# A state-space block and a mixture of experts on one core: the first block's rows spread by TensorE, softplus from the absolute value, the branch ahead of the projection

## The chip, the cores and the metric

The kernel runs on one core of a Trainium2 chip. The metric is device time in microseconds, the median of several executions. One further execution was recorded by the hardware profiler; every profile line below is from that one. The engines are PE (TensorE, matrix products), DVE (VectorE), ACT (ScalarE), POOL (GpSimd) and SP (SyncE, which here issues nearly all transfers).

## The reference

The input x is 4 sequences of 1024 tokens with 128 channels. Two layers follow, each added to its input and normalised. The first is a selective state-space layer:

```python
xz = einsum('bld,ed->ble', x, in_proj_w)          # 512 = 2 x 256 channels
xb, z = xz[..., :256], xz[..., 256:]
xb = silu(conv_b + sum over 4 taps of xpad[:, k:k+Lq] * conv_w[:, k])
proj = einsum('bld,ed->ble', xb, x_proj_w)        # 33 rows: dt_in, 16 of B, 16 of C
dt = softplus(dt_in * dt_w[:, 0] + dt_b)
dA = exp(dt[..., None] * A)                       # A = -exp(A_log), 16 states a channel
x_scaled = (xb * dt)[..., None] * Bp[..., None, :]
h[t] = dA[t] * h[t-1] + x_scaled[t]               # written as an associative scan
y = einsum('bldn,bln->bld', h, Cp) + xb * D_param
y = layernorm(y) * ln_g + ln_b;  y = y * silu(z);  out = y @ out_w.T
```

The second is a causal attention with 16 heads of 8 channels, then a mixture of 16 experts (128 to 512 to 128, gelu, two experts a token, limited capacity).

## The kernel before

**Two plans.** The kernel is written as a list of operations, each with a due time `v`, the engines that could do it and an estimated duration. `Plan.schedule` (L194) simulates the engines: when one is free it takes, among the operations whose inputs are done and whose buffers are free, the one with the lowest `v`. `Plan.run` (L337) emits the instructions in that order. Engines take their instructions strictly in order, so a misjudged order makes an engine wait on the chip, while idle time in the plan itself is not emitted. An ACT operation that needs another function table than the loaded one gets 100 added to its `v`. Where the plan sees a gap of 800 ns or more on PE while an accumulation group is open, it sends groups of four matmuls by zeros (`fill`, L1556), one group for each 550 ns of gap.

`plan_a` (`before_branch`, L1451) holds the work ahead of a branch; the second plan (`mild_path`, L1518) all the rest. The branch tests one number, `mild`: a bound on the attention scores that is worked out from the weights (`pn`, `nrm`, `pbound`, `most`, L1475 to L1499, with a power on POOL and due times 9 and 10). The other side of the branch is a slower path that is not run here.

**Fronts.** Tokens are taken in eight halves of a sequence, 512 tokens each. `front(f, v, step)` (L1403) computes for one half, channels on partitions: `conv` (four taps as matmuls with the weights `w_tap`) and its Silu `xb`; `zmm` and its Silu `sz`; `xproj` and a copy `proj`; the product `dtmm` with `w_dt`. Then softplus for each of two groups of 128 channels: `dtmin` on DVE (add the bias, limit to 40), Exp, Ln(1 + .) on ACT, and the maximum with the argument on DVE (`dt`); then `u` = xb times dt. All of xb, sz, the B and C rows (`bc_d`), dt and u are written to DRAM. Front 0 stands in `plan_a`, the seven others in the second plan with due times 18 to 112. `front_w` matrices, A_log and the small vectors are loaded at the very start, A_log by ACT's queue (L1504).

**Scans.** `scans(u)` (L1652) takes a unit of 512 (at the end 256) tokens. For a block `m` of 128 channels it reads dt and u back so that 32 channels lie on 128 partitions, each repeated for 4 of the 16 states (`u_sp`, `dt_sp`, four transfers of 256 KB each), and the B and C rows repeated over channels. For each of four state groups: `uB` on DVE, four decays `da` = Exp(a_neg * dt) on ACT (five buffers), four `scan` on DVE, `hC` on DVE, and `py` on PE, which sums over states.

**The rest.** `norm_and_inputs` (L1733) does the layer norm, the gate and the output product, and q, k, v for attention in three bf16 parts each; its powers (`rs_pow`, `lnx_pow`) run on POOL. `attention` (L1804) runs at a lag of 60 to 90 in due time behind the scans; its tiles lie over the fronts' buffers, so it starts when the last front is done. Five of its tiles get 64 rows cleared on POOL (`pad`, L2025, due at 100). `post` (L1868) ends the layer and prepares token rows (`xrow`, with a token number from POOL in the last column); `route` sends rows to experts; the experts follow.

The operation helpers of class `Emit` record every operation under a few lines: L390 is every matmul, L417 every activation, L437 every tensor_tensor, L463 every scan, L450 a tensor_scalar of two operations (`dtmin` among them), L457 a scalar_tensor_tensor, L368 every plain transfer.

Of the kernel before, what the change touches and what calls it, by code (L numbers as in the profile page):

```python
# [9 lines left out]
F32 = mybir.dt.float32  # L10
# [8 lines left out]
P = 128  # L19
# [36 lines left out]
TABLE = 1283  # L56
# [81 lines left out]
class Op:  # L138
    __slots__ = ("v", "engs", "emit", "deps", "succ", "left", "ready", "start", "end", "done", "eng", "allocs",
                 "uses", "table", "name", "wire", "seq", "opens", "closes")  # L140


class Plan:
# [17 lines left out]
    def add(self, v, engs, emit, outs, ins, name="", table=None, wire=0, free=(), after=()):  # L161
# [3 lines left out]
        op.opens = op.closes = None  # L165
        op.start = op.end = op.done = op.eng = None
# [27 lines left out]
    def schedule(self):  # L194
# [65 lines left out]
        times, queued = [0.0], {0.0}  # L260

# [7 lines left out]
        while n_left:  # L269
# [8 lines left out]
            while again:  # L278
                again = False
                for e in engines:  # L280
# [3 lines left out]
                    for op in waiting[e]:  # L284
# [6 lines left out]
                        if e == "ACT" and op.table and op.table != table:  # L291
                            v += 100.0
                        if best is not None and (v, op.seq) >= best[:2]:
                            continue
# [23 lines left out]
                    op.end = t + dur  # L318
                    op.done = op.end
# [17 lines left out]
    def run(self):  # L337
        order = self.schedule()
        last, ready, groups = 0.0, False, {}
        with self.tc.manual_schedule():  # L340
            for op in order:
                if op.eng == "PE":
                    gap = op.start - last
                    if ready and groups and gap >= FILL_GAP:
                        view = next(iter(groups.values()))
                        for _ in range(int(gap / FILL_STEP)):
                            self.fill(view)
                    last = op.end
                op.emit(op.eng)
                ready = ready or op is self.fill_after  # L350
                if op.opens is not None:
                    groups[id(op.opens.buf)] = op.opens
                if op.closes is not None:
                    groups.pop(id(op.closes.buf), None)


class Emit:
# [12 lines left out]
    def pe(self, v, calls, share=1, name="", group=None, last=False):  # L370
        nc = self.nc
        dur, outs, ins = 0.0, [], []
        for kind, out, lhsT, rhs, start, stop in calls:
# [7 lines left out]
            dur += one / 0.92 / share  # L381
            outs.append(out)
# [9 lines left out]
        op = self.p.add(v, {"PE": dur}, emit, outs, ins, name)  # L392
        if group is not None:
            op.opens, op.closes = (None, group) if last else (group, None)
# [34 lines left out]
    def _dve(self, v, emit, outs, ins, cols, per=1.0, fixed=None, name="", pool=False):  # L429
        if fixed is None:  # L430
            fixed = 125 if any(x.psum for x in outs + ins) else 62
        return self.p.add(v, {"POOL" if pool else "DVE": (fixed + per * cols / 0.96) * (2.2 if pool else 1)}, emit, outs, ins, name)

    def tt(self, v, out, a, b, op, pool=False, name=""):
        eng = self.nc.gpsimd if pool else self.nc.vector
        fixed = 600 if op == ALU.pow else None
# [41 lines left out]
    def memset(self, v, out, value, pool=False, name=""):  # L478
        eng = self.nc.gpsimd if pool else self.nc.vector
        return self._dve(v, lambda e: eng.memset(out.real(), value), [out], [], out.cols, name=name, pool=pool)  # L480
# [15 lines left out]
def mamba_then_moe_block_kernel(ctx: ExitStack, tc: tile.TileContext, a: dict, out: bass.AP):  # L496
# [847 lines left out]

    plan_a = Plan(nc, tc)
# [36 lines left out]
    conv_b, dt_b = small("f_conv_b", [P, NC2]), small("f_dt_b", [P, NC2])  # L1382
# [8 lines left out]
    def fronts_of(p, e, n_dt):  # L1391
# [9 lines left out]
        W = dict(w_in=fx(w_in), w_tap=fx(w_tap), w_xp=fx(w_xp), w_dt=fx(w_dt), conv_b=fx(conv_b), dt_b=fx(dt_b))  # L1401

        def front(f, v, step):  # L1403
# [9 lines left out]
            xb = []  # L1413
            for c in range(NC2):
                pt = p.new(pool["bank"])
                e.pe(v + step, [
# [4 lines left out]
                e.act(v + 2 * step, t, pt, AF.Silu, bias=W["conv_b"][:, c : c + 1], name="xb")  # L1421
                e.dma(v + 7 * step, fx(chan["xb"][f])[c * P : (c + 1) * P, :], t, name="xb_d")
                xb.append(t)
            for c in range(NC2):
                pt = p.new(pool["bank"])
                e.pe(v + 2 * step, [("mm", pt, W["w_in"][:, DI + c * P : DI + (c + 1) * P], xT[:, NTAP - 1 :], True, True)], name="zmm")
                t = p.new(pool["sz"])
                e.act(v + 2 * step, t, pt, AF.Silu, name="sz")
                e.dma(v + 6 * step, fx(chan["sz"][f])[c * P : (c + 1) * P, :], t, name="sz_d")
            pt = p.new(pool["bank"])  # L1430
            e.pe(v + 3 * step, [("mm", pt, W["w_xp"][:, c, :], xb[c], c == 0, c == NC2 - 1) for c in range(NC2)], name="xproj")
            proj = p.new(pool["proj"])
            e.act(v + 3 * step, proj, pt, AF.Copy, name="proj")
            e.dma(v + 4 * step, fx(bc_h[f]).rearrange("s g i t -> (s g i) t"), proj[1 : 1 + 2 * NS, :], name="bc_d")
            for c in range(NC2):
# [3 lines left out]
                b1 = W["dt_b"][:, c : c + 1]  # L1439
                e.ts(v + 4 * step, ex, pt, b1, DT_MAX, ALU.add, ALU.min, name="dtmin")  # L1440
                e.act(v + 5 * step, ex, ex, AF.Exp, name="sp_exp")
                e.act(v + 5 * step, ex, ex, AF.Ln, bias=fx(one_col), name="sp_ln")
                dt = p.new(pool["dt"])
                e.stt(v + 6 * step, dt, pt, b1, ex, ALU.add, ALU.max, name="dt")
                e.dma(v + 6 * step, fx(chan["dt"][f])[c * P : (c + 1) * P, :], dt, name="dt_d")
                u = p.new(pool["u"])
                e.tt(v + 6 * step, u, xb[c], dt, ALU.mult, name="u")
                e.dma(v + 6 * step, fx(chan["u"][f])[c * P : (c + 1) * P, :], u, name="u_d")
        return front

    def before_branch():  # L1451
        p, e = plan_a, ea
        fx = p.fixed
        for t, value in ((mean_col, 1.0 / DI), (one_col, 1.0), (neg_half, -0.5)):
            e.memset(0, fx(t), value, name="memset")
        def load(v, t, src, queue="SP"):
# [11 lines left out]
        load(2.2, w_dt, fx(a["dt_w"]))  # L1468
        load(2.3, dt_b, fx(a["dt_b"]).rearrange("(n p) -> p n", p=P))
        for k in range(NTAP):  # L1470
            e.tt(2, fx(w_tap)[:, k, :], fx(w_in)[:, 0:DI], fx(conv_w)[:, :, k], ALU.mult, name="w_tap")
        front = fronts_of(p, e, 2)
        front(0, 0.5, 2.5)

        pn = ps.single[0][:, 0:8].rearrange("p (t s g) -> p t s g", t=2, s=2)  # L1475
        for s, w in enumerate((wq_pad, wk_pad)):
            sqw = fx(bnd[s])
            e.ts(3, sqw, fx(w), fx(ln1_w), None, ALU.mult, name="sqw")
            e.tt(3, sqw, sqw, sqw, ALU.mult, name="sqw")
            for g in range(GQ):  # L1480
                e.pe(9, [("mm", fx(pn)[:, 0, s, g : g + 1], sqw[:, g, :], fx(one_col), True, True),
# [754 lines left out]
```

## Time and profile before

| what | value |
|---|---|
| timed executions, median of 3 | 1115.01 us (1114.6 to 1119.04) |
| profiled execution, its own time | 1093.94 us |
| its span, first to last instruction | 1092.1 us |
| mean granted clock of PE | 0.914 |
| first scan begins | 47.60 us |
| last scans end | about 768 us |
| first expert matmul | 920.39 us |
| last transfers and norm | 1047 to 1092 us |

Times inside the execution count from the span's start. In the lines of the timeline the columns are start, duration, engine, line, operation, output and inputs; "x4" counts instructions, and the bracket holds the idle time of that engine ahead of them and what ended it. In lists of waits the numbers are microseconds in total, times, and the longest.

### The profile page before, as it was taken

Reading aid. Unit: us, or ns where it says so; the run is one execution under the profiler, and the core shown is the slowest. Engines: PE = TensorE matmul, PEld = TensorE weight load, DVE = VectorE, ACT = ScalarE, POOL = GpSimd, SP = SyncE. Lnnn points to the kernel's source line nnn. Section 1 sums busy time; section 2 is a strip of 40 time slices with the busy share of each in tenths; the row PEclk is TensorE's granted clock in tenths of the full one; section 3 lists DMA queues with packets and bytes.
Section 4 is the critical chain, followed back from the end, with each engine's and each line's share of the span. In section 5 each row is a group of like instructions: output and inputs, shape, how many; then the busy total and the mean of one; then the engine's idle time right before and its main releaser. Section 6 shows DMA issues by size and latency. Waiting matters only on the chain.

```text
span 1092.1 us, 16985 instructions
## 1 busy us (share of the span) xinstructions
PE 891.0 (82%) x6090; PEld 446.7 (41%) x6136; DVE 793.4 (73%) x1390; ACT 708.1 (65%) x1069; POOL 233.4 (21%) x337
## 2 busy tenths in 40 slices
PE   6378879577899999899999899999889964999910
PEld 2123324224334324543433543434455532777710
DVE  2477889998999999999999999999524221111146
ACT  3376687354898897788799679898656742334311
POOL 2020001300001000182100263000060303555532
PEclk9589989778999999899999989999999975999965
DMA  3776587575754644374555466345943302322162
GB/s 104 254 189 217 180 285 247 175 217 179 233 134 136 215 136 131 123 226 145 181 152 148 123 189 169 91 144 159 306 125 94 109 12 78 119 86 68 40 170 84
DMA packets 152757, 168.65 MB, mean 154 GB/s; under 512 B 23635, under 2 KB 105814, under 8 KB 152534
## 3 DMA queue, kind: packets, MB, share of 16 engines
q1 hardware_dynamic: 146262, 158.63, 48.4%
q0 software_dynamic: 4096, 8.43, 2.2%
q8 instruction: 50, 0.82, 0.3%
q10 hardware_dynamic: 2304, 0.40, 0.2%
q14 instruction: 45, 0.37, 0.1%
HBM read 110.20 MB, written 57.21 MB: 153 GB/s over the span
## 4 chain that ended last, share of the span: by engine, by line
PE 48%; DVE 24%; ACT 10%; DMA 7%; issue 7%; POOL 2%; SPq 1%; DVEq 0%; ACTq 0%; POOLq 0%
PE bank L390 25%; PE pair L390 20%; DVE arena L463 10%; DVE arena L437 10%; ACT arena L417 8%; DVE arena L457 2%; PE bank L388 2%; SPq L368 1%; DMA arena<-in_fc_w_dram 1%; DMA arena<-q_parts 1%; DVE smalls L487 1%; DMA q_parts<-halves 1%; POOL smalls L437 1%; DMA eout<-rt_full 1%; DMA k_parts<-halves 1%
## 5 line engine op out<-in xcount | busy, mean ns | idle before, releaser
L417 ACT ACTIVATE arena<-pair 128x1024 f32<-128x1024 f32 (+2 forms) x336 | 299.1, 923 | 66.7 <-PE pair L390 57.0
L437 DVE TENSOR_TENSOR arena<-arena 128x2048 f32<-128x2048 f32 (+2 forms) x155 | 305.7, 1991 | 11.9 <-DMA arena<-u_h 11.9
L417 ACT ACTIVATE arena<-arena,f_a_neg 128x512 f32<-128x512 f32 (+1 forms) x288 | 187.8, 675 | 82.4 <-DVE arena L463 68.2
L390 PE MATMUL pair<-arena 128*128 128x256 bf16 (+3 forms) x821 | 184.0, 309 | 25.1 <-ACT arena L417 17.6
L437 POOL TENSOR_TENSOR smalls<-smalls,neg_half 128x4 f32<-128x4 f32 (+2 forms) x35 | 54.0, 1544 | 598.5 <-DVE smalls L448 531.7
L390 PE MATMUL bank<-arena,vp 128*32 128x256 f32 (+3 forms) x1728 | 165.6, 465 | 2.9 <-ACT arena L412 1.3
L463 DVE TENSOR_TENSOR_SCAN arena<-arena,state 128x512 f32<-128x512 f32 (+1 forms) x160 | 160.9, 1054 | 0.0
L463 DVE TENSOR_TENSOR_SCAN arena<-arena 128x512 f32<-128x512 f32 x128 | 150.1, 1209 | 0.1
L390 PEld LDWEIGHTS <-arena 128*128 128x128 bf16 x864 | 79.0, 98 | 155.3 <-issue 132.9
L2010 POOL DMA_INDIRECT xin<-xrow,rt_put x64 | 83.1, 1299 | 82.0 <-issue 34.6
L390 PE MATMUL bank<-arena,f_sel 128*32 128x512 f32 x512 | 72.6, 643 | 30.2 <-DVE arena L437 30.0
L390 PE MATMUL pair<-mask_k,identb 128*128 128x128 bf16 x512 | 95.3, 220 | 1.6 <-issue 0.8
L417 ACT ACTIVATE arena<-pair,b 128x512 f32<-128x512 f32 x64 | 40.5, 684 | 71.4 <-PE pair L390 71.4
L390 PE MATMUL pair<-xT,f_w_tap 128*128 128x512 f32 x128 | 64.2, 651 | 21.7 <-DMA xT<-in_xT_dram 17.8
L2111 POOL DMA_INDIRECT eout<-arena,to x64 | 61.3, 957 | 67.5 <-DVE arena L437 56.8
L390 PEld LDWEIGHTS bank<-arena,vp 128*32 128x32 f32 x1728 | 38.2, 109 | 59.7 <-issue 45.2
L417 ACT ACTIVATE arena<-arena,smalls 128x128 f32<-128x128 f32 x73 | 30.3, 483 | 49.3 <-DVE smalls L457 45.1
L390 PEld LDWEIGHTS bank<-arena 128*128 128x128 f32 x512 | 59.8, 192 | 5.6 <-issue 4.3
L390 PE MATMUL bank<-arena 128*128 128x128 f32 x512 | 61.2, 277 | 0.5 <-ACT arena L417 0.4
L437 DVE TENSOR_TENSOR arena<-bank,arena 128x512 f32<-128x512 f32 (+1 forms) x25 | 16.7, 666 | 60.6 <-PE bank L390 60.6
L388 PE MATMUL bank<-ident,arena 128*128 128x128 f32 x256 | 42.3, 291 | 21.5 <-DMA arena<-xin 15.9
L390 PE MATMUL pair<-arena,arena 128*128 128x512 f32 x128 | 59.4, 608 | 0.0
(184 smaller groups left out, 1082.7 us busy)
## 6 DMA issues: line engine op xcount, KB each, us to landing
arena<-k_parts SPq DMA_DIRECT2D x52, 288.0 KB
arena<-bc_h SPq DMA_DIRECT2D x56, 256.0 KB
arena<-dt_h SPq DMA_DIRECT2D x56, 256.0 KB
arena<-u_h SPq DMA_DIRECT2D x56, 256.0 KB
arena<-in_fc_w_dram SPq DMA_DIRECT2D x32, 256.0 KB
q_parts<-halves SPq DMA_DIRECT2D x21, 384.0 KB
k_parts<-halves SPq DMA_DIRECT2D x21, 384.0 KB
arena<-q_parts SPq DMA_DIRECT2D x28, 288.0 KB
```

The costliest lines, as they stand in the source:

```text
L368: return self.p.add(v, {queue: 460}, lambda e: engine.dma_start(out.real(), in_.real()), [out], [in_], name, wire=wire, after=after)
L388: nc.tensor.transpose(out.real(), lhsT.real(), rhs.real())
L390: nc.tensor.matmul(out.real(), lhsT=lhsT.real(), rhs=rhs.real(), start=start, stop=stop)
L417: nc.scalar.activation(out.real(), in_.real(), func, scale=real(scale), **kw)
L437: return self._dve(v, lambda e: eng.tensor_tensor(out.real(), a.real(), b.real(), op), [out], [a, b], out.cols, fixed=fixed, name=name, po ...
L457: return self._dve(v, lambda e: nc.vector.scalar_tensor_tensor(out.real(), a.real(), real(s), b.real(), op0, op1), [out], self._views(a, s ...
L463: return self._dve(v, lambda e: nc.vector.tensor_tensor_scan(out.real(), d0.real(), d1.real(), real(init), ALU.mult, ALU.add), [out], self ...
L487: self._dve(v, lambda e: nc.vector.bn_stats(s.real(), x.real()), [s], [x], 128, name=name + "_bn")
L2010: inst = nc.gpsimd.indirect_dma_start(out=dst.real()[:, :], out_offset=bass.IndirectOffsetOnAxis(ap=idx.real(), axis=0), in_=src.real(), i ...
L2111: inst = nc.gpsimd.indirect_dma_start(out=eo_d.real()[:, :], out_offset=bass.IndirectOffsetOnAxis(ap=idx.real(), axis=0), in_=src.real(), ...
```

## The change

The change has these parts.

1. `front` is split into `conv_half` (conv, xb, zmm, sz) and `dt_half` (xproj to u). Front 0's `conv_half` stays ahead of the branch; its `dt_half` moves behind it, where `adopt` takes over the two xb buffers. The chain of `mild` gets due times of 1.8 to 2.9.
2. Softplus is max(x, 0) + ln(1 + exp(-|x|)). The bias dt_b becomes a row of `w_dt`, with a matching row of ones that the copy of `proj` adds; `dtmin` goes, and an Abs on ACT takes its place.
3. Block m = 0 of unit 0 no longer goes through DRAM: eight matmuls by a 0/1 matrix (`wide`) spread dt and u over partitions into PSUM. The first state group's decays and `uB` read PSUM; eight copies (`spread_c`, ACT or DVE) fill the tiles for the other three groups. Front 1's conv waits for the last of these matmuls and its gates for the last of these decays.
4. A_log is loaded by SP's queue; its Exp waits for the second gate of front 0.
5. The planner: a function of another table must have been ready for 3 us before it is taken (`HOLD`); PE is counted at half speed in windows of 3413 ns that follow one with little work (`Clock`); the costs of a power and a memset on POOL change; fillers are also sent before the first attention product, into a spare bank, in both plans.
6. The pads are due at 150 instead of 100, and the token column is written ahead of `x2`.

```diff
-TABLE = 1283
+TABLE, HOLD = 1283, 3000
+SPAN, ENOUGH = 3413.0, 3000.0
...
+class Clock:
...
+    def slow(self, k):
+        return self.work.get(k - 1, 0.0) < ENOUGH
...
+    def fill(self, t, gap, n):
+        for i in range(n):
+            k = int((t + (i + 0.5) * gap / n) / SPAN)
+            self.work[k] = self.work.get(k, 0.0) + 512.0
...
                         if e == "ACT" and op.table and op.table != table:
                             v += 100.0
+                            if t < op.ready[e] + HOLD:
+                                wake(op.ready[e] + HOLD)
+                                continue
...
+                    if e == "PE":
+                        gap = t - last
+                        if ready and (groups or spare) and gap >= FILL_GAP:
+                            op.fillers = int(gap / FILL_STEP)
+                            clock.fill(last, gap, op.fillers)
+                            op.filled = next(iter(groups.values()), None)
+                        spare = spare and op.name != "av"
+                        op.end = last = clock.end(t, dur, op.work)
...
-        fixed = 600 if op == ALU.pow else None
+        fixed = 620 + 63 * out.cols if op == ALU.pow else None
...
+    def filler(p, spare):
+        def fill(view):
+            n = spare.cols if view is None else view.cols
+            to, some = (spare if view is None else view).real(), some_b.unsqueeze(1).to_broadcast([P, n // P, P])
+            for j in range(4):
+                nc.tensor.matmul(to[32 * j : 32 * j + 32, :], lhsT=zero_b, rhs=some, start=view is None, stop=view is None)
...
-            e.act(v + 3 * step, proj, pt, AF.Copy, name="proj")
+            e.act(v + 3 * step, proj, pt, AF.Identity, bias=fx(ident)[:, 1 + 2 * NS : 2 + 2 * NS], name="proj")
...
-                b1 = W["dt_b"][:, c : c + 1]
-                e.ts(v + 4 * step, ex, pt, b1, DT_MAX, ALU.add, ALU.min, name="dtmin")
-                e.act(v + 5 * step, ex, ex, AF.Exp, name="sp_exp")
+                e.act(v + 4 * step, ex, pt, AF.Abs, name="sp_abs")
+                e.act(v + 5 * step, ex, ex, AF.Exp, scale=-1.0, name="sp_exp")
                 e.act(v + 5 * step, ex, ex, AF.Ln, bias=fx(one_col), name="sp_ln")
                 dt = p.new(pool["dt"])
-                e.stt(v + 6 * step, dt, pt, b1, ex, ALU.add, ALU.max, name="dt")
+                e.stt(v + 6 * step, dt, pt, 0.0, ex, ALU.max, ALU.add, name="dt")
...
-        front(0, 0.5, 2.5)
+        conv_half(0, 0.5, 2.5)
...
-        e.act(21, a_all, a_all, AF.Exp, name="a_all")
+        e.act(21, a_all, a_all, AF.Exp, name="a_all").deps.add(conv_half.last[1][1])
...
+        xb_first = [adopt("xb") for _ in range(NC2)]
+        first = dt_half(0, 0.0, 2.0, xb_first, kept=(0,))
...
+                    if spread:
+                        wide = new("tmp", "wide")
+                        e.copy(1, wide.rearrange("p (m i) -> p m i", i=NI), fx(ident).unsqueeze(2).to_broadcast([P, P, NI]), name="wide")
+                    for j in range(J if spread else 0):
+                        lhsT = wide[:, j * P : (j + 1) * P]
+                        for src, dst, k in ((first[0][0], dts[j], 0), (first[0][1], us[:, j, :], 1)):
+                            pb = new("bc")
+                            mm = e.pe(12 + 0.1 * j + 0.05 * k, [("mm", pb, lhsT, src, True, True)], name="spread")
+                            if k:
+                                e.tt(12 + 0.1 * j, h[:, j, :], pb, bt[g], ALU.mult, name="uB")
+                            else:
+                                d_first.append(new("da"))
+                                ex = e.act(12 + 0.1 * j, d_first[j], pb, AF.Exp, scale=fx(a_neg)[:, j, 0:1], name="da")
+                            e.act(14 + j, dst, pb, AF.Copy, dve=True, name="spread_c")
+                    for conv, gate in second_front if spread else ():
+                        conv.deps.add(mm)
+                        gate.deps.add(ex)
...
-                e.memset(100, rest[64:P, :], 0.0, pool=True, name="pad")
+                e.memset(150, rest[64:P, :], 0.0, pool=True, name="pad")
```

`Clock.end`, not shown, divides a matmul's duration by one half while `slow` holds.

## The prediction

> **What bounds the kernel now.** I read the page first, then busy time by stage, the timeline of the start, and the waits of VectorE (DVE) while the projections run.
>
> ```profile
> span 1092.1 us, 16985 instructions
> PE 891.0 (82%) x6090; PEld 446.7 (41%) x6136; DVE 793.4 (73%) x1390; ACT 708.1 (65%) x1069; POOL 233.4 (21%) x337
> ```
>
> No engine is full on average, so the stages decide (columns: PE, PEld, DVE, ACT, POOL busy, granted PE clock, DMA share, GB/s):
>
> ```profile
> 0.00:45.00 45.00, 18.59 (x48) 8.17 (x48) 10.65 (x38) 14.36 (x19) 6.49 (x26) 0.75 0.47 146
> 75.00:132.00 57.00, 48.46 (x139) 18.27 (x138) 45.45 (x50) 42.66 (x56) 0.20 (x2) 0.92 0.58 193
> ...
> 304.00:390.00 86.00, 80.28 (x577) 33.31 (x584) 85.51 (x94) 74.78 (x110) 6.53 (x4) 1.00 0.53 160
> ...
> 800.00:860.00 60.00, 55.92 (x586) 33.76 (x585) 19.83 (x106) 39.95 (x56) 22.68 (x42) 1.00 0.36 105
> ```
>
> Until 45 us nobody is busy: a latency chain. From 304 to 734 DVE is 95% to 99% busy in every stage (85.51 of 86 in the one shown): the scans. After their end near 770 PE works off the attention that is left (55.92 of 60), then the experts. Attention of a block needs its scans, and the experts need the last attention; so what DVE gains before attention starts (about 255) should reach the end whole. The start:
>
> ```profile
> 17.84 0.69 ACT L417 ACTIVATE arena<-pair,f_conv_b 128x512 f32<-128x512 f32 x1 [7.12 <-PE pair L390]
> 18.55 1.28 ACT L409 ACT_TABLE_LOAD   x1
> 19.84 0.31 ACT L417 ACTIVATE arena<-arena 128x128 f32<-128x128 f32 x1
> 20.17 1.28 ACT L417 ACT_TABLE_LOAD   x1
> 21.46 0.69 ACT L417 ACTIVATE arena<-pair,f_conv_b 128x512 f32<-128x512 f32 x1
> ...
> 37.51 2.48 SPq L368 DMA_DIRECT2D arena<-u_h  x4
> ...
> 45.21 2.29 DVE L437 TENSOR_TENSOR arena<-arena 128x2048 f32<-128x2048 f32 x1 [11.86 <-DMA arena<-u_h]
> ...
> 47.60 4.57 DVE L463 TENSOR_TENSOR_SCAN arena<-arena 128x512 f32<-128x512 f32 x4
> ```
>
> The two gates of the convolution are torn apart by an Exp that needs another table, and DVE then waits 11.86 us for rows that were written to DRAM (dt from 31.08, u from 32.34) and are read back spread out. DVE's waits from 45 to 205 us:
>
> ```profile
> DVE arena L450 <- PE pair L390: 14.7, 4, 5.6
> DVE arena L437 <- DMA arena<-u_h: 11.9, 1, 11.9
> DVE arena L457 <- ACT arena L417: 3.9, 4, 2.1
> DVE arena L450 <- ACT arena L417: 2.7, 1, 2.7
> ```
>
> L450 is `dtmin`, one small pass that stands on DVE ahead of the scans and waits for a projection that PE has not done.
>
> **The start, step by step.** The convolution still ends near 17.8: the weight load and w_tap (8.96 to 11.17) gate it, and no edit shortens those. Gates at 17.84 and 18.5, done 19.1 instead of 22.15, since Exp of A_log now waits for the second gate. Its table load (1.28) and Exp (0.31) end at 20.7; nobody needs a_neg before 28. The branch now lies here: in the chain of waits it took 0.25 on DVE and 0.65 on SP; ACT at 21.2. Its condition chain is ahead of the projection and has PE, DVE and POOL idle around it; its longest part is the power on POOL (1.01). Projection copy 0.59: 21.8. Two dt products: 1.98 (the four-pass row at 68.21); 23.8. On ACT, Abs twice, Exp twice, one Ln: Abs isn't in the trace; bounds are the 0.58 of a copy out of PSUM and the 0.69 of a biased one; I take 0.60. That is 1.2 + 1.25 + 0.66: 26.9. dt 0.70: 27.6; u 0.65: 28.3. Spreading product: 128x128 by 128x512 f32, 0.88 warm (half of a two-pass 1.02 to 1.98 row gives 0.86 to 0.99). First decay 28.5 to 29.4, u's product ends 29.4, multiplication by B out of PSUM 0.69: first scan at about 30.4 instead of 47.60. The others come at the pace of the two banks: PE 1.8 per pair, DVE 0.69 + 1.15 and perhaps a copy of 0.6, ACT 0.7 and a copy or two: 2.2 us each. Four scans end at 30.4 + 6.6 + 1.2 = 38.2 instead of 52.1: **14 us**. The copies and `wide` (0.6, ahead of need) are in that pace. Ten 256 KB transfers vanish (two writes, eight spread reads), so the B and C rows that are queued behind them on SP now (from 40.67) come sooner; B's first row needs the projection's write and one read, some 5 us after 21.8, ahead of 29.4.
>
> Here a rule speaks against the sum. Row: eight py matmuls at 213.19 took 1.93 us, after sixty filling matmuls that began at 203.09 and lasted 5.40, and 4.71 us of idleness; warm, at 161.24, eight took 1.07. The Trainium skill ("TensorE: Matmul & The Clock Gate", Part 1: The HAM clock gate) says that the array drops to half rate after an idle window of about 3.4 us. The changed planner counts fillers as spread over a gap, while the code sends them in a block at its head; the rule says that a long gap still ends cold. Between dt products and spreading the gap is 3.8 us: six groups, then at least 2 us idle, under the window. So warm by both, narrowly; if cold, dt products are 3.8 instead of 2.0 and spreading twice as slow, +1.8 and about +5: the start is then worth 7.
>
> **The fronts, 45 to 205 us.** `dtmin` goes: sixteen passes, two of them in the first block; fourteen at 0.70 (1.41 for two) = **9.9 us** of DVE in its own bound. In its place ACT gets fourteen Abs at 0.60 = 8.4 us. ACT is busy for about 108 of these 160 us, so that lies beside DVE; without that cover it costs up to 8.4. Abs would cost far more if it forced a table load; the Trainium skill ("ScalarE: Activation LUTs", Table sets: the hidden batching unit) puts abs in every set, which no run here shows.
> `dtmin`'s stalls (14.7 + 2.7 = 17.4 us) needn't vanish: a late projection now stops ACT, with the decays queued behind Abs, and `dt` on DVE waits for ACT. Five decay buffers (some 5.8 us of scans) are the cushion. Bounds 0 and 17; I take **5**, nearer to the lower end because only a better plan removes lateness.
> The holding rule (a function of another table waits 3 us in the plan) gathers gates. Rows: 35 loads of 1.28, nearly all before 190. Halving them frees about 20 us of ACT. The same page (What ACT_TABLE_LOAD costs) adds a drain of 1.38 to each, which would make it 42; but the Exp at 19.84 starts as the load of 18.55 ends, so 20. ACT isn't the bound there: counted as 0.
>
> **Edits at nothing.** The second front's convolution waits for the last spreading product (about 37); behind it on PE stand its z product and projections, and ACT's gates wait for it. It stood at 45.99 before, so nothing is lost. A_log's eight loads move from ACT's queue (9.75 to 14.93) to SP's, before any write there is urgent; two more weight rows add 0.4 each; both are over by 15. The five clearings (1.8 each, 189.99 to 200.65) move behind the first block's second power. There the power waited 4.63 for DVE after them; k and q tiles are loaded from 239.69, some 20 us after the new end. Without that cover: 9. The token column is 0.42 on POOL, ahead of x2, with POOL idle most of the time. New planning costs of power and clear reorder later work; the trace cannot show it: bounds -6 and +6, value 0.
>
> **Sum.** 14 + 9.9 + 5 = 28.9 of the profiled execution's 1093.94 (span 1092.1 and 1.84 around it): 1065. The timed median, 1115.01, is 1.9% above that execution, with nothing in the profile to say why; I keep the saving in us: **1086**.
>
> **Rivals.**
> *Only a part arrives* (0.34). PE is cold when it spreads (7), or the stalls only move to ACT (0 instead of 5), or later work is reordered badly. Smallest sums: 7 + 9.9 - 6 = 11; typical 16: about 1099. For it: PE's clock of 0.75 up to 45, and the cold row at 213.19. Against: the short gaps.
> *It doesn't do what it says* (0.07): the start is quick, but attention begins no earlier, because clear-out transfers (DVE waited 2.2 for one) and the norm hold it; within 5 us of 1115. Against: DVE has no idle 86-us stage after that in which a shift could be lost.
> *Holding starves the scans* (0.09). The place: decays and gates share ACT. When a gate batch comes, the decays behind it wait for convolution, two loads (2.56) and four gates (2.6); DVE has five decays in stock. If each of seven fronts stops DVE for 5 us more, 35 us are lost against 28.9: 1121. It decides above 4.1 us a front. For it: DVE already waits for ACT's part of the front, 3.9 us in four places (L457). Against: ACT waited 14.5 us for DVE's buffers in the same stretch, so decays run ahead.
>
> **The numbers.** Forecast 0.50, at 1086 with its own range 1074 to 1096. A change under 0.5% (5.6 us) is about what a measurement of this kernel can't tell from none. Faster 0.84, same 0.07, slower 0.09. The range 1070 to 1109 takes in the partial case and leaves out the last two and a thin lower end, where all stalls vanish (17 instead of 5).
>
> **What would show it.** First scan near 30 and the fourth ending near 38; no wait on u's rows; 128x512 spreading products of 0.45 a pass; no L450 group with 16 passes; DVE busy over 9 tenths from 75 to 205; fewer than 25 table loads; scans ending near 739, the first expert product (920.39 now) near 891. If the first scan is early but that product stays at 920, the carrying through is wrong; if DVE waits long for ACT between 40 and 190, the holding rule ate it; if spreading passes take 0.85, the clock was cold.

## The result, and the profile after

| what | before | after |
|---|---|---|
| timed executions, median of 4 | 1115.32 us (1114.6 to 1119.04) | 1098.04 us (1096.94 to 1102.41) |
| ratio after to before, 95% interval | | 0.9846 (0.9811 to 0.9881) |
| two later comparisons, on two chips | 1123.07 and 1117.49 | 1096.93 and 1095.33: 0.9788 (0.9742 to 0.9833) and 0.9789 (0.9743 to 0.9834) |
| profiled execution, own time | 1093.94 | 1098.80 |
| first scan; the 16th; the last ends | 47.60; 97.2; 768 | 34.88; 73.9; 754.7 |
| table loads | 35 | 19 |

The change makes the kernel faster by 17.3 us in the first comparison and by 26.1 and 22.2 in the later ones (differences of medians; the two later ratios put both near 24). The forecast was 28.9. The profiled execution of before came out 1.9% under its own timed executions, and that of after did not, so the ends of these two profiles can't be subtracted; where stages are compared below, a second profile of the kernel before (1088.91, from a chip that runs it in 1092) stands beside them.

The head of the page of after, and the four stretches that were shown of before (columns: PE, PEld, DVE, ACT, POOL busy, granted PE clock, DMA share, GB/s):

```profile
span 1097.4 us, 17033 instructions
PE 902.9 (82%) x6111; PEld 450.2 (41%) x6156; DVE 784.6 (71%) x1383; ACT 696.0 (63%) x1073; POOL 226.6 (21%) x337
...
0.00:45.00 45.00, 35.71 (x132) 14.63 (x133) 20.56 (x52) 17.88 (x28) 7.87 (x33) 0.96 0.60 177
75.00:132.00 57.00, 50.08 (x155) 19.01 (x154) 48.06 (x47) 41.71 (x60) 0.10 (x1) 0.94 0.77 256
304.00:390.00 86.00, 77.48 (x561) 32.71 (x560) 85.31 (x80) 73.95 (x110) 5.52 (x3) 0.98 0.53 159
800.00:860.00 60.00, 45.27 (x420) 25.43 (x420) 14.86 (x84) 31.45 (x45) 14.34 (x27) 0.86 0.28 81
```

DVE does twice the work in the first 45 us (20.56 instead of 10.65), and PE's clock there is 0.96 instead of 0.75. From 75 to 132 DVE is busier than before, but still idle for 9 of 57 us, where the prediction wanted over nine tenths. The scans from 304 on are as full as they were. From 800 to 860 PE is now idle for 15 us of 60; that is taken up at the end.

The start in the timeline of after:

```profile
19.56 0.69 ACT L454 ACTIVATE arena<-pair,f_conv_b 128x512 f32<-128x512 f32 x1 [3.79 <-PE pair L426]
20.26 1.28 ACT L446 ACT_TABLE_LOAD   x1
...
28.39 0.48 DVE L485 TENSOR_SCALAR w_out_b<-w_out,ln_b 128x128 f32<-128x128 f32 x2 [4.58 <-DMA ln_b<-in_ln_b_dram]
...
29.51 0.38 PE L426 MATMUL bank<-one_col,arena 1*128 1x1 f32 x2 [3.21 <-POOL arena L513]
...
29.82 4.63 PE L426 MATMUL bank<-arena,arena 128*128 128x512 f32 x6
...
34.16 0.69 DVE L474 TENSOR_TENSOR arena<-bank,arena 128x512 f32<-128x512 f32 x1 [0.88 <-ACT arena L449]
...
34.88 1.22 DVE L500 TENSOR_TENSOR_SCAN arena<-arena 128x512 f32<-128x512 f32 x1
...
44.55 2.33 DVE L500 TENSOR_TENSOR_SCAN arena<-arena 128x512 f32<-128x512 f32 x2
```

Two small constants of later stages stand in the way. DVE waits 4.58 us for `ln_b` to make `w_out_b`; `dt` of the first block, whose Ln ended at 26.64, stands behind it and is done at 29.47. PE waits 3.21 us for POOL ahead of the bias product `pbias`, which begins at 29.51. The spreading products stand behind both, so either one alone would have held them to about 29.5. They then take 4.63 us for six passes, 0.77 each. The first scan is 12.7 us earlier than before, not 17.2. The fourth is the first of the pair at 44.55: `uB` of the next group (2.28 at 42.35) was placed ahead of it. It ends at 45.8 where 38.2 was forecast.

DVE's waits from 45 to 205 us:

```profile
DVE arena L494 <- ACT arena L454: 11.1, 8, 2.8
DVE arena L494 <- issue: 3.3, 1, 3.3
DVE arena L474 <- PE bank L426: 1.3, 1, 1.3
DVE arena L494 <- PE pair L426: 1.2, 1, 1.2
```

The waits of `dtmin` for PE (14.7) and for u's rows (11.9) are gone. In their place `dt` (L494) waits for ACT, 11.1 us in eight places instead of 3.9 in four (L457 then).

### The profile page after: what moved, and what is told of

Its sections match the earlier page's. It is cut to its first block, busy times and chain, and to the rows that moved or that the text cites. A ratio compares the mean times of both kernels' runs of the same rounds, so it can differ in the third digit from the quotient of the medians.

```text
span 1097.4 us, 17033 instructions
## 1 busy us (share of the span) xinstructions
PE 902.9 (82%) x6111; PEld 450.2 (41%) x6156; DVE 784.6 (71%) x1383; ACT 696.0 (63%) x1073; POOL 226.6 (21%) x337
## 4 chain that ended last, share of the span: by engine, by line
PE 40%; DVE 28%; ACT 11%; issue 8%; DMA 7%; POOL 3%; SPq 2%; another core or an unknown queue 2%; ACTq 0%; DVEq 0%; POOLq 0%
PE bank L426 19%; PE pair L426 18%; DVE arena L500 12%; DVE arena L474 10%; ACT arena L454 9%; DMA xin<-rt_full 2%; PE bank L424 2%; SPq L403 2%; DVE arena L494 2%; POOL xin L2111 2%; DVE smalls L539 1%; DMA arena<-q_parts 1%; DVE rt_full L474 1%; DMA xin<-xrow,rt_put 1%
## 5 line engine op out<-in xcount | busy, mean ns | idle before, releaser
L454 ACT ACTIVATE arena<-pair 128x1024 f32<-128x1024 f32 (+2 forms) x352 | 307.6, 907 | 121.9 <-PE pair L426 94.3
L454 ACT ACTIVATE arena<-arena,f_a_neg 128x512 f32<-128x512 f32 (+1 forms) x284 | 184.2, 674 | 68.2 <-DVE arena L500 51.7
L426 PE MATMUL pair<-arena 128*128 128x256 bf16 (+3 forms) x824 | 187.2, 313 | 36.9 <-ACT arena L454 24.2
L474 POOL TENSOR_TENSOR smalls<-smalls,neg_half 128x4 f32<-128x4 f32 (+2 forms) x35 | 57.6, 1646 | 633.2 <-DVE smalls L485 568.8
L426 PE MATMUL bank<-arena,vp 128*32 128x256 f32 (+3 forms) x1728 | 168.2, 474 | 10.4 <-ACT arena L454 3.6
L2111 POOL DMA_INDIRECT xin<-xrow,rt_put x64 | 78.0, 1219 | 71.8 <-DVE smalls L485 26.8
L426 PE MATMUL bank<-arena,f_sel 128*32 128x512 f32 x512 | 70.2, 624 | 11.9 <-DVE arena L474 11.3
L474 DVE TENSOR_TENSOR arena<-bank,arena 128x512 f32<-128x512 f32 (+1 forms) x29 | 19.4, 670 | 78.6 <-PE bank L426 77.7
L424 PE MATMUL bank<-ident,arena 128*128 128x128 f32 x256 | 45.1, 301 | 32.5 <-DMA arena<-xin 15.2
L426 PE MATMUL pair<-xT,f_w_tap 128*128 128x512 f32 x128 | 58.0, 597 | 0.6 <-ACT arena L454 0.6
```

Of the source, the lines that this page charges most:

```text
L424: nc.tensor.transpose(out.real(), lhsT.real(), rhs.real())
L426: nc.tensor.matmul(out.real(), lhsT=lhsT.real(), rhs=rhs.real(), start=start, stop=stop)
L454: nc.scalar.activation(out.real(), in_.real(), func, scale=real(scale), **kw)
L474: return self._dve(v, lambda e: eng.tensor_tensor(out.real(), a.real(), b.real(), op), [out], [a, b], out.cols, fixed=fixed, name=name, po ...
L2111: inst = nc.gpsimd.indirect_dma_start(out=dst.real()[:, :], out_offset=bass.IndirectOffsetOnAxis(ap=idx.real(), axis=0), in_=src.real(), i ...
```

## The experiments

The kernel before is timed beside each; a ratio is to it, with its 95% interval. Chips differ: the first four runs are from one that runs the kernel before in 1092 us, the others from two that take 1123 and 1117. One measure returns: DVE's busy time from the start to the beginning of the 48th scan and of the 80th. The rest of such a stretch is idle time. Savings in us are differences of medians; those that follow from the ratios differ from them by up to 3 us.

**1. The kernel before, again.** No edit.

> The kernel before, unchanged, for a second profile and as the measure of what no change looks like. Theory 1 (the profiled execution of before was an unusually quick one and the gain of the change is real in every stage): time 1113 to 1118, and a profile whose span is some 20 us longer than 1092 with the same order of instructions, scans ending near 775 to 785 instead of 768 and the first expert product near 935 instead of 920. Theory 2 (that profile is typical, and timed executions lose time outside the span): span near 1092 again.

Measured: 1091.75 us, ratio 0.9999 (0.9981 to 1.0016), span 1087.1, last scans end at 762.4. Of theory 2 the span holds, but not that timed executions lose time outside it: on this chip they agree with the profile. Theory 1 fails. Since the same kernel takes 1092, 1117 and 1123 us on three chips, the likely reading is that the first profile and the first timing came from different chips; which chips those were isn't recorded.

**2. The first block's rows through DRAM.**

```diff
-        first = dt_half(0, 0.0, 2.0, xb_first, kept=(0,))
+        first = dt_half(0, 0.0, 2.0, xb_first, kept=())
...
-                own = u == 0 and m == 0
+                own = False
```

> The kernel after, with the first front's dt and u written to DRAM and read back spread as before; everything else of the change stays. Theory 1 (the spreading brings a first scan 12 us earlier in the profile and that is carried to the end): 8 to 13 us slower than after, 1106 to 1111, first scan near 45 to 48. Theory 2 (what the start gains is given back before the experts, since attention loses it again): within 4 us of after, 1094 to 1102.

Measured: 1081.06 us, 0.9909 (0.9881 to 0.9938). The hold on the second front went with the spreading, and its convolution overtook the first front's dt product: first scan at 56.5, 10 us later than before. Yet the kernel is 11.2 us faster than before. So a good part of the gain doesn't hang on an early start; how large a part this run can't say, since the kernel after wasn't timed on this chip and the second front's hold changed too.

**3. `dtmin` on DVE again, in place of Abs.**

```diff
-                e.act(v + 4 * step, ex, pt, AF.Abs, name="sp_abs")
-                e.act(v + 5 * step, ex, ex, AF.Exp, scale=-1.0, name="sp_exp")
+                e.ts(v + 4 * step, ex, pt, DT_MAX, None, ALU.min, name="dtmin")
+                e.act(v + 5 * step, ex, ex, AF.Exp, name="sp_exp")
...
-                e.stt(v + 6 * step, dt, pt, 0.0, ex, ALU.max, ALU.add, name="dt")
+                e.stt(v + 6 * step, dt, pt, 0.0, ex, ALU.add, ALU.max, name="dt")
```

> The kernel after, with softplus by the minimum on DVE and the maximum at the end instead of Abs on ACT; the bias stays a row of the product, so that only the one pass of DVE comes back: sixteen passes of about 0.70. Theory 1 (those passes lay in DVE's own bound and their stalls with them): 10 to 15 us slower than after, 1108 to 1113. Theory 2 (the stalls only moved to ACT's Abs and the pass lay in DVE's idle time): 0 to 5 us slower, 1098 to 1103.

Measured: 1077.75 us, 0.9896 (0.9854 to 0.9938), that is 14.5 us faster than before without this part. The kernel after wasn't timed beside it, so it was repeated:

> The kernel after with the minimum back on DVE in place of Abs on ACT, beside after on one chip. Theory 1 (sixteen passes of 0.70 and their stalls lay in DVE's own bound, as the prediction counted: 9.9 and 5): 10 to 15 us above after. Theory 2 (between 75 and 304 us DVE waits for ACT about as long as it saved, so the pass only filled idle time): within 4 us of after. The profile's DVE waits for ACT between 75 and 218 (L494) should then be near 1 us instead of 9 to 17.

Measured: 1095.76 us, beside 1095.33 for after; ratios 0.9806 (0.9765 to 0.9847) and 0.9789 (0.9743 to 0.9834). Theory 2. The two runs of this kernel also answer what `after_third` asks: it saves 14.5 us on the chip that runs the kernel before in 1092 and 21.7 on the one that takes 1117, and the intervals of the two ratios don't touch. Part of what is saved depends on the chip. Its waits of DVE from 45 to 205:

```profile
DVE arena L485 <- PE pair L426: 9.9, 4, 4.3
DVE arena L494 <- PE pair L426: 1.3, 1, 1.3
DVE arena L494 <- PE bank L426: 1.3, 1, 1.3
DVE arena L494 <- ACT arena L454: 0.7, 1, 0.7
```

With `dtmin` (L485) DVE stands 9.9 us for the projection; without it (the view above) `dt` stands 11.1 us for ACT. The stall moved whole. And since `dtmin` still stands 9.9 us here, of 14.7 before, the rest of the change shortened that wait by a third. DVE's busy time to the 48th and the 80th scan, first in the second profile of before, then in that of after from the same chip as this kernel, then in this kernel (columns: length of the stretch, DVE busy, granted clock, DMA share, GB/s):

```profile
0.00:205.10 205.10, 149.01 (x183) 0.87 0.67 215
0.00:289.70 289.70, 229.44 (x264) 0.85 0.66 208
```

```profile
0.00:183.20 183.20, 140.31 (x174) 0.96 0.72 224
0.00:272.00 272.00, 220.79 (x256) 0.91 0.69 213
```

```profile
0.00:185.80 185.80, 150.15 (x192) 0.96 0.71 223
0.00:269.40 269.40, 228.23 (x273) 0.93 0.68 212
```

Busy time falls by 8.7 us from before to after (149.0 to 140.3), where sixteen passes make 11.3; spreading added work on DVE. Put back, they cost 9.8 of busy time at the 48th scan, but idle time is 35.7 instead of 42.9: three quarters of the passes fill time in which DVE would stand anyway. At the 80th scan the kernel with the passes is 2.6 us ahead.

**4. No holding.**

```diff
-TABLE, HOLD = 1283, 3000
+TABLE, HOLD = 1283, 0
```

> The kernel after, with the planner's holding of functions of another table set to 0 instead of 3000 ns. Theory 1 (ACT is not the bound, as the prediction counted): within 3 us of after, 1095 to 1101, with 30 to 35 table loads instead of 19. Theory 2 (holding keeps decays late and hurts the scans): 5 us or more faster, below 1093. Theory 3 (the saved loads are what made the gain): 8 us or more slower, above 1106.

Measured: 1071.88 us, 0.9832 (0.978 to 0.9884), 29 table loads. Repeated beside after:

> The kernel after with the holding set to 0, beside after on one chip. Theory 1 (a queue of held functions delays projections and decays; the mended pair differed by 11 us): 6 to 11 us faster than after. Theory 2 (that pair differed by the order of later work that the change of plan happened to bring): within 4 us of after.

Measured: 1092.39 us, 0.976 (0.9722 to 0.9798), 2.9 under after; the intervals overlap. Theory 2 of the repeat. Ten more loads of 1.28 cost nothing that shows. DVE waits longer for ACT in `dt` without holding (16.8 us, longest 6.4, from 45 to 205), and the kernel is no slower: taken alone, holding is worth about nothing here. Experiment 7 shows that this depends on what else is changed.

**5. The kernel after, again.**

> The kernel after, unchanged, beside the kernel before on one chip, since single edits were timed on a chip that runs the kernel before in 1092 instead of 1115 us. Theory 1 (the partial gain is a property of the change): ratio to before 0.983 to 0.987, some 15 to 18 us, with the 48th scan about 21 us ahead of before and the last scans about 16 to 18 us ahead, as in the kernel without holding. Theory 2 (the first result lost about 8 us to waits on the far side of transfers near 560 to 660 us, which this profile will lack): ratio 0.975 to 0.979, 23 to 27 us.

Measured: 1096.93 us, 0.9788 (0.9742 to 0.9833). Neither as written: the ratio is that of theory 2, but the profile still has the far-side waits (6.1 us at 623, 5.3 at 781, 10.5 at 837). And a third time, with the repeated edits:

> The kernel after once more, so that the two single edits below stand beside it on one chip. Two earlier comparisons gave 0.985 and 0.979 of before. Theory A (the gain is a fixed saving of about 17 to 20 us whatever the chip): 0.980 to 0.985. Theory B (what a chip adds to the kernel before is partly spared by the change): 0.984 or more on a chip that runs the kernel before in 1092, 0.979 or less on one that takes 1120.

Measured: 1095.33 us, 0.9789 (0.9743 to 0.9834). On these chips the saving is 22 to 26 us. Theory B's other half, after on a chip that runs the kernel before in 1092, wasn't run; the two runs of experiment 3 speak for it.

**6. Late constants out of the first block's way.**

```diff
+        first_scan = [o for o in p.ops if o.name == "scan"][3]
+        for o in p.ops:
+            if o.name in ("w_out_b", "pbias", "qkb", "identb", "neg_identb"):
+                o.deps.add(first_scan)
```

> The kernel after, with the products w_out_b (DVE), the small bias products (PE) and the casts of the identity held behind the fourth scan, so that nothing that waits for a late constant stands ahead of dt, u and the spreading products. Theory 1 (these waits made the first scan 4 us late and turned PE cold, and scans ahead reach the end): first scan near 31 to 32, first spreading products under 1 us each, 2 to 5 us faster than after. Theory 2 (what the first scans gain is taken back before the 16th, since by then fronts and not scans set the pace): first scan earlier, but within 2 us of after at the end.

Measured: 1098.97 us beside 1096.93 for after; 0.9806 (0.9765 to 0.9847). Theory 2. The first two spreading products take 0.99 us each and the first scan begins at 31.4, 1.7 us earlier than in the profile of after from the same chip (33.1). By the second scan the lead is gone (36.5 against 35.1): PE's clock is 0.50 from 31.5 to 34.8, and the next six passes take 0.77 each. So this run doesn't test what a lead that lasts would be worth. But its 48th scan is 11.1 us behind that profile (191.2 against 180.1), its last ones end 1.5 behind (750.6 against 749.1), and its median is 2.0 behind. A lead at the 48th scan doesn't reach the end by itself.

**7. The same without holding.**

> As the mended one, with the planner's holding set to 0 as well. Theory 1 (the two add): 2 to 5 us faster than the one without holding, which stood at 0.983 of before: 0.979 to 0.981. Theory 2 (any gain at the start is lost in the fronts): 0.983 again, within 0.002.

Measured: 1087.60 us, 0.9695 (0.9656 to 0.9734), 9.3 under after and 11.4 under the mended kernel with holding; neither theory's ratio. Repeated on another chip:

> Both mendings, beside the one without holding on one chip. Theory 1 (earlier scans add their 4 us): 2 to 5 us faster than without holding alone. Theory 2 (a lead at the first scans is made even by the 48th): within 2 us of it. Either way faster than after by 5 to 10 us, if the first result of this version (0.9695 of before) holds.

Measured: 1089.65 us, 0.974 (0.9695 to 0.9785), 5.7 under after and 2.7 under the kernel without holding. That is theory 1 by the medians, but the intervals overlap. This version has the lowest median of both comparisons; only in the first is it clear of after by its interval. Its start:

```profile
26.73 0.69 DVE L494 SCALAR_TENSOR_TENSOR arena<-pair,arena 128x512 f32<-128x512 f32 x1 [3.14 <-ACT arena L454]
...
27.47 1.98 PE L426 MATMUL bank<-arena,arena 128*128 128x512 f32 x4 [1.12 <-DVE arena L494]
...
31.55 0.69 DVE L474 TENSOR_TENSOR arena<-bank,arena 128x512 f32<-128x512 f32 x1 [0.90 <-DMA arena<-bc_h]
```

`dt` follows the first Ln at once, spreading is warm, and the next limit shows: the row of B, whose write goes out on SP at 24.81 and whose reads begin at 28.60, among loads of constants. Which of the two edits makes the gain isn't settled: mending alone gave none, no holding alone 2.9, and most of the 11 us between the medians of the two mended kernels doesn't show in their profiles (the last scans end 3.4 apart, 750.6 and 747.2, the profiled executions 4.9).

**8. Through DRAM, with the second front held.** As 2, but the second front's convolution waits for the first front's dt product and its gates for the first front's last Ln.

```diff
+            if second_front is None:
+                for conv, gate in conv_half.last:
+                    conv.deps.add(first_dt)
+                    gate.deps.add(first_ln)
```

> The kernel after with the first front's rows through DRAM, as in the earlier experiment, but with the second front's convolution held behind the first front's dt product and its gates behind the first Ln, so that the first front isn't overtaken (there the first scan began at 56.5). Theory 1 (spreading is worth its lead at the first scans): first scan at 42 to 46, 8 to 10 us later than in after, and the time 8 to 10 us above after. Theory 2 (fronts set the pace between the 16th and 48th scan, so most of a late start is made up there): at most 5 us above after.

Measured: 1101.56 us beside 1096.93 for after; 0.9807 (0.9771 to 0.9843). The first scan began at 55.7, so the hold didn't give the start that theory 1 wanted; 22 us of lateness cost 4.6. Theory 2 by the median. DVE's busy time to the 48th and 80th scan:

```profile
0.00:189.50 189.50, 137.57 (x170) 0.92 0.73 232
0.00:275.70 275.70, 218.05 (x251) 0.91 0.69 217
```

Against the profile of after from the same chip it is 22.6 us late at the first scan, 9.4 at the 48th (180.1) and 8.7 at the 80th (267.0). These two profiled executions end 14.8 apart, the medians 4.6 and the ratios 2, with overlapping intervals. So 22.6 us of lateness at the first scan cost some 2 to 9 us here. It isn't a clean price for the start, since the second front's convolution begins at 24.9 in this kernel and at 39.2 in that profile of after, and may give some of it back. Without spreading the 48th scan still leads the second profile of before by 15.6 us (189.5 against 205.1), where after leads by 21.9 to 25.0: most of the lead at that scan can be had without it.

## Why the prediction was right, and where it was not

The time lay inside the range, at the value of the rival that let only a part arrive (1099), and 2 us above the forecast's own range. The sum of 28.9 was too high by 3 to 12, and its terms were not what the runs show. The terms with a value, start, `dtmin` and stalls, brought some 2 to 9 us when undone alone; the rest of the gain is not traced to any of them, and edits that stood in the sum at nothing are likely to hold part of it. So the number is in part luck.

**The start, 14.** First scan at 34.9 instead of 30.4. Up to the first Ln the sum held (it ends at 26.6, forecast 26.9). The failing step is "dt 0.70: 27.6" and what follows: the list of instructions ahead of `dt` and of the spreading left out what the planner puts there, `w_out_b` on DVE and `pbias` on PE. The rule of the Trainium skill weighed there ("TensorE: Matmul & The Clock Gate", Part 1: The HAM clock gate) was read as "warm, narrowly", with at least 2 us of idleness after the fillers. The granted clock speaks against that reading, already in the row that the prediction took from the kernel before. First the time behind that row's fillers, which end at 208.5, then the time behind the fillers of after, which end at 26.3 (columns: PE, PEld, DVE, ACT, POOL busy, granted PE clock, DMA share, GB/s):

```profile
208.50:210.50 2.00, 0.00 (x0) 0.00 (x0) 2.00 (x3) 0.72 (x1) 0.00 (x0) 1.00 0.35 132
210.50:213.20 2.70, 0.01 (x2) 0.01 (x2) 2.70 (x4) 0.00 (x0) 0.00 (x0) 0.50 0.33 75
```

```profile
26.30:29.50 3.20, 0.00 (x1) 0.00 (x0) 1.08 (x3) 1.58 (x3) 0.83 (x4) 1.00 0.35 110
30.00:33.00 3.00, 3.00 (x4) 0.87 (x4) 1.98 (x5) 0.69 (x1) 0.00 (x0) 0.50 0.90 287
```

In the kernel before, the clock was halved 2.0 us after the last filler. In after twenty fillers were sent (1.26 us from 25.04), `w_out_b` and `pbias` stretched the idleness to 3.21 us, and the clock was 0.50 for the first passes of the spreading. Both pauses were under the 3.4 of the rule, so here the measurement decides: a shorter pause was enough. The six passes took 0.77 each instead of 0.45 (0.50 where experiment 6 has them warm). The pace of 2.2 us a scan was 2.0 to 3.0, and the fourth came last behind the next group's `uB`. Its end, from which the 14 was worked out, is 6.4 us earlier than before (45.8 against 52.2); with that `uB` done, the fifth scan begins 13.0 earlier (45.7 against 58.7).

As far as experiment 8 prices it, the larger error is in the carrying: it begins its scans 22.6 us after the kernel after and ends 2 to 9 later. DVE isn't in its own bound this early. "What DVE gains before attention starts should reach the end whole" was read from the stages after 304, where DVE is full, and applied to a stretch where DVE idles for 43 of 183 us.

**`dtmin`, 9.9, and its stalls, 5.** The busy time fell by 8.7 to the 48th scan, somewhat less than forecast. Its worth is 0.4 us in the timed pair, with an uncertainty of some 6. Here the failing step is "in its own bound": the row of waits shown beside it said the opposite, since `dtmin` stood 14.7 us for PE and 2.7 for ACT. What the prediction named as the danger, a late projection that stops ACT while `dt` on DVE waits for it, is what happened: 11.1 us. The value of 5 should have been none, and the two terms should not have been added, because here the work removed in front of a wait only lengthened the wait. Abs itself forced no table load: in after it runs at 24.29 and 25.45 with an Exp at 24.92 between and no load among them, 0.58 to 0.60 us each.

**Edits at nothing.** Holding, counted 0: 0 to 3 us of loss in the kernel after, and 11 between the medians of the mended kernels. The load count (19, under 25) was as forecast. Of the branch and the second front the prediction said "it stood at 45.99 before, so nothing is lost", and looked no further. In the timeline of before that line reads:

```profile
40.03 0.59 SPq L368 DMA_DIRECT2D xT<-in_xT_dram  x1
...
45.99 9.14 PE L390 MATMUL pair<-xT,f_w_tap 128*128 128x512 f32 x16 [17.78 <-DMA xT<-in_xT_dram]
```

PE stood 17.78 us for the tokens of the second front. Their load belongs to the plan behind the branch, and stood there behind the spread reads of dt and u, which waited for their writes. In after, the branch comes earlier:

```profile
21.32 0.81 SPq L403 DMA_DIRECT2D xT<-in_xT_dram  x2
...
40.92 7.03 PE L426 MATMUL pair<-xT,f_w_tap 128*128 128x512 f32 x16
```

In every changed kernel, those that go through DRAM too, the first of these loads begins between 19 and 26 us, and PE waits at most 2.2 us for them. In after the convolution is tied to the last spreading product and begins only 5.1 us earlier. But PE's clock from 45 to 75 rises from 0.84 to 1.00, the sixteen passes take 7.03 us instead of 9.14, and the second front's first `dt` comes at 63.6 instead of 77.1. In the two kernels through DRAM the convolution begins at 23.1 and 24.9. This fits that each part taken alone costs little when it is undone: an earlier second front remains in all of them. It is a reading of the profiles; no run moved the branch alone, so its share isn't measured. The planner's count of the clock and A_log's queue weren't run alone either and stay rivals. Two edits can be ruled out. The clearings on POOL lay at 189.99 to 200.65, while after has its lead of 22 to 25 us by its 48th scan at 180 to 183. And of the fillers none lies between 26.3 and 75 us in after, so they don't hold the clock there.

**Carried through to the end.** For the kernel without holding that step held. On the chip that ran 1 and 4 its 48th scan is 20.4 us ahead of before, the last scans 17.2 and the end of the span 16.6. For the kernel after it held in part. Its three profiles, two of them from the slower chips, lead the second profile of before by 22 to 25 us at the 48th scan, by 16 to 23 at the 200th (578 to 585 against 601) and by 8 to 13 at the last (749 to 755 against 762; forecast 739). In each of the three, DVE stands near 630 us in one wait that the profile can't name, here in the second:

```profile
DVE arena L494 <- remote: 6.5, 1, 6.5
```

It is 5.0 and 4.9 us in the other two, and no other profile has it on DVE there. "DVE has no idle 86-us stage after that in which a shift could be lost" is what failed: from 562 to 648 DVE of after is busy for 76 to 79 us, before for 82 to 84. The first products of the experts follow a wait for their rows that ends at 923.9 in after and at 917.9 before, not near 891. By the prediction's own sign the carrying would be wrong altogether. But the waits of the last section lie ahead of that point too; in the kernel without holding, on the chip of 1 and 4, it comes at 898.2, 15.4 ahead of before there.

**Rivals.** "Only a part arrives" was the one, for two of its three reasons: PE cold at spreading, and stalls moved to ACT. Its third, bad reordering, isn't ruled out: the wait near 630 is in every profile of after and in none of the kernels that differ from it by one planner constant. "Holding starves the scans" fell for after: `dt`'s longest wait for ACT is 2.8 us, under the 4.1 from which it was to decide. One sum of the prediction doesn't fit its text: stalls that vanish whole (17 instead of 5) give 1074, which lies inside the range and not below it.

## What to carry to other kernels

A pass taken off a busy engine is worth its duration only where that engine's next instruction doesn't wait: look at the row of waits before adding a busy time to a sum, and never count a pass and the stall behind it as two gains. For a row that seems to lose nothing, read its bracket: 17.78 us of waiting for a transfer behind a branch was a hint that the prediction passed over. When lateness at the start is to be priced, price it at the first stage that is full, by the idle time of the stages between.

## What the runs showed of the hardware

The same kernel (without holding) took 1071.88 us on one chip and 1092.39 on another. In their profiles the last scans end 4.8 us apart, but the experts' first table load comes at 902.2 and at 925.6. Two stretches of the first and then of the second (columns as above):

```profile
800.00:825.00 25.00, 23.40 (x206) 14.52 (x206) 8.93 (x47) 15.04 (x27) 1.04 (x2) 0.90 0.30 83
825.00:850.00 25.00, 24.83 (x289) 14.12 (x287) 8.05 (x48) 17.99 (x21) 9.08 (x16) 1.00 0.33 99
```

```profile
800.00:825.00 25.00, 15.81 (x105) 9.18 (x106) 1.74 (x6) 11.96 (x19) 6.48 (x13) 0.74 0.27 81
825.00:850.00 25.00, 19.82 (x232) 11.88 (x232) 11.15 (x73) 13.68 (x20) 8.20 (x15) 1.00 0.36 105
```

PE loses 12.6 us in these 50. The chain of work of the second names what it can't see (start, duration):

```profile
796.08 3.80 another core or an unknown queue
...
800.99 7.54 another core or an unknown queue
...
842.55 10.45 another core or an unknown queue
```

The first chip's chain has none of these. Every profile of a changed kernel from the slower chips has such waits, and the first profile of after with them: the idle time of PE that it shows from 800 to 860 goes with them (without holding, on the first chip, PE is busy for 58 of those 60 us). What releases them isn't recorded, and why chips differ stays open. One practical point follows: a profile and a timing from different chips can differ by as much as the change.

A second one is the clock of a PE that is nearly idle. In the mended kernel four spreading passes at 25.81 took 1.98 us, and the next six, at 31.57 after 1.12 us of work and two pauses of 0.65 and 2.01, took 4.60: 0.50 and 0.77 each, in one kernel, within 6 us. The granted clock is 1.00 for the first four, and 0.50 from 31.5 to 34.8. In the repeat of the mended version without holding the same pauses were 0.65 and 1.68, and the clock stayed at 1.00 (27.4 to 36.5).
